# A diagonal LSTM and a small quantum circuit: the resident ring is laid out by runs of eight rows of an image

## The chip, the cores and the metric

The kernel runs on one core of one Trainium2 chip. The metric is the device time in microseconds (us) of one execution; lower is better. Tensors are float32.

## The reference

x has 16 images of 128 channels and 64 x 64 points. Two layers are added to it, each on a group-normalised input (32 groups of four channels):

```
# layer 1: a recurrence along diagonals (rows are skewed: row i is shifted right by i)
xs  = skew(gn(x))                          # 127 columns
i_s = w_is @ xs + b_is                     # 4 gates of 128 channels
for each column t:
    gates = i_s[t] + w_ss[:, :, 0] @ h_of_the_row_above + w_ss[:, :, 1] @ h + b_ss
    o, f, i = sigmoid(...); g = tanh(...)
    c = f * c + i * g;  h = o * tanh(c)
x = x + unskew(h)
# layer 2: at every point, 128 channels -> 4 angles -> circuit of 4 qubits -> 4 values -> 128 channels
x = x + post_w @ simulate(pre_w @ gn(x) + pre_b, q_weights) + post_b
```

## The kernel before

The 128 channels are the partitions. An image has 64 rows of 64 points, 16 KB in a partition, and 16 images are 256 KB, more than fits. So 40 rows of each image stay in an SBUF tile, `ring`, and 24 pass through it in turn. A block is four rows of one image, BLOCK = 256 numbers (1 KB in a partition). `ring` is a tile of [128, 10, 16, 256]: block by block, in each block the 16 images side by side. `block(r)` names the block of row r: rows 32 to 39 lie in blocks 0 and 1, rows 0 to 31 in blocks 2 to 9, and rows 40 to 63 later in blocks 2 to 7. A chunk is 512 numbers, eight rows, in two blocks.

**First stage, loads and statistics (L243 to L430).** For each image, `rows` loads the five chunks of the ring (L246, 80 transfers of 256 KB in all) and `behind` the other three into spare tiles (L259, 48). VectorE takes the statistics of each chunk when it has landed (L283). Beside this, `inv_step` runs 33 serial steps of the recurrence on a state with no input (matmuls L194, activations L197 to L205, products on GpSimd L200 to L202); its results start rows at the border. After the last image come the first products of the gates, three matmuls on loaded rows (`keep`, L177), the group mean (L142) and the inverse root.

**The scan (160 steps, `step`, L743).** All work is ordered by hand. Two bands of 32 rows go along the diagonals, the second 65 steps behind the first. Step t works on one column of each active row: `now`, `new` and the other states have a column per row and image, even rows in one half (q = 0), odd rows in the other, by pairs j. TensorE multiplies by the gates' weights (L583 for the input, L752 for the states); ScalarE and VectorE do the gates. GpSimd, in this order in each step: the differences between neighbouring rows (L605, L608), which TensorE's products need; `residual` (L617), which adds the step before's result to x in the ring; `normalised` (L564, L569, L574), which takes the diagonal of x two steps ahead out of the ring and normalises it. Both walk the ring with `diagonal` (L527): one operation takes a run of row pairs j with all 16 images, and the run is cut where the address pattern demands it. With row blocks of four, a pattern holds an even number of pairs that begins at an even one, and a pair left over at either end is an operation of its own.

When four rows are finished, they are saved to DRAM if the place is needed again (`low`, L629, six times 2 MB), VectorE takes their statistics for the second layer (L705), and then the place is refilled with four further rows of x (L712, six times 2 MB).

**Last stage, the second layer (L956 to the end).** For each image, two halves: angles (L976), sine, the circuit's amplitudes (L1005), squares (L1018), the output product (L1027). `finish` adds the product to the rows on VectorE (L1046) and SyncE sends each chunk to DRAM (L1047). Rows 0 to 23 come back out of `low` into freed places by GpSimd's DMA queue (`load`, L860). Images go in order; the loads run some images ahead.

Of the kernel before, what the change touches and what calls it, by code (L numbers as in the profile page):

```python
# [11 lines left out]
F32 = mybir.dt.float32  # L12
# [4 lines left out]
P = 128  # L17
NB = 16
NH = 64
NW = 64  # L20
# [3 lines left out]
RING = 40  # L24
ROWS = 4
BLOCK = ROWS * NW
CHUNK = 2 * BLOCK
EARLY = 33
FIRST = 8
STRIP = 4  # L30
FEW = 96
LEAST = 128
AHEAD = RING - SLOTS
BAND = NW + 1
# [46 lines left out]
def kernel(  # L81
# [17 lines left out]
    xv = x.rearrange("b c h w -> b c (h w)")  # L99
    ov = out.rearrange("b c h w -> b c (h w)")  # L100

    const = ctx.enter_context(tc.tile_pool(name="const", bufs=1))
# [3 lines left out]

    ring = const.tile([P, RING // ROWS, NB, BLOCK], F32, name="ring")
    NLOW = NH - RING  # L110
    NT = NLOW * NW // CHUNK
    low = dram.tile([NB, P, NLOW * NW], F32, name="low")
# [19 lines left out]
    w_out = const.tile([P, 128], F32, name="w_out")  # L132
    b_out = const.tile([P, 1], F32, name="b_out")

    def block(r):

        return (r + AHEAD if r < SLOTS else r - SLOTS) // ROWS

    def group_mean(psum, v, mean, which, scale):

# [15 lines left out]
    with ExitStack() as scan:  # L156
# [17 lines left out]
        def keep(pool, tag, v):  # L174

            ps = pool.tile([P, v.shape[-1]], F32, name=nc.get_next_instruction_name(), tag=tag)
            nc.tensor.matmul(ps, lhsT=wsT[:, 0:P], rhs=v, start=True, stop=True)  # L177
# [37 lines left out]
        with ExitStack() as prep:  # L215
# [5 lines left out]
            ps_keep = prep_ps.enter_context(tc.tile_pool(name="ps_keep", bufs=1, space=PSUM))  # L221
# [19 lines left out]
            rests = {}  # L241

            def rows(b):  # L243
                for k in ORDERED:
                    at = (2 * k * ROWS - AHEAD) * NW if k else SLOTS * NW
                    nc.sync.dma_start(  # L246
                        out=ring[:, 2 * k : 2 * k + 2, b, :],
                        in_=xv[b, :, at : at + CHUNK].rearrange("c (k n) -> c k n", n=BLOCK),
                    )

            def behind(b):
# [11 lines left out]
            for i in range(2):  # L263
                nc.scalar.dma_start(out=ws_n[i], in_=ws_v[:, 2 * i : 2 * i + 2])
            nc.scalar.dma_start(
                out=qw, in_=q_weights.rearrange("l w a -> (l w a)").partition_broadcast(P)
# [12 lines left out]
            nc.gpsimd.memset(cinv[:, 0:1], 0.0)  # L279

            def statistics(b, k):
                v = ring[:, 2 * k : 2 * k + 2, b, :] if k < 5 else rests[b][k - 5]
                nc.vector.bn_stats(stats[:, b, k, :], v)  # L283

            def aggregated(b):
# [69 lines left out]
            for i in range(2):  # L355
                v = ws_n[i]
# [14 lines left out]
            for b in range(NB):  # L371
                while b < NB - 1 and done * (NB - 1) < EARLY * (b + 1):
                    inv_step(done, ps_inv)
                    keep(ps_keep, "keep", ring[:, 2, b, 0:P])
                    keep(ps_keep, "keep", wsT[:, 0:P])
                    if done == 0:

                        transposed("wxT", wxT, lambda g: wx_n[:, g, :])
                        transposed("w0T", w0T, lambda g: ws_n[g // 2][:, g % 2, 0::2])
                        transposed("w1T", w1T, lambda g: ws_n[g // 2][:, g % 2, 1::2])  # L380
                    elif done > 4 and between:
                        between.pop(0)()
                    done += 1
                if b + 2 < NB:
                    rows(b + 2)
                if b + 1 < NB:
                    behind(b + 1)
                    for k in ORDERED:
                        statistics(b + 1, k)
                for k in (5, 6, 7):  # L390
                    statistics(b, k)
                aggregated(b)
# [134 lines left out]
        def diagonal(t, band, q, j0, j1):  # L527


            j = j0  # L530
            while j < j1:
                odd = (j + AHEAD // 2 * (1 - band)) % 2
                n = 1 if odd or j + 1 == j1 else (j1 - j) // 2 * 2
                r = 2 * j + q + AHEAD * (1 - band)
                at = r // ROWS * NB * BLOCK + r % ROWS * NW + t - BAND * band - 2 * j - q
                dims = [[BLOCK, NB]]
                if n > 1:
                    dims = [[NB * BLOCK - ROWS, n // 2], [2 * NW - 2, 2]] + dims
                yield j, n, bass.AP(origin.tensor, origin.offset + at, [list(origin.ap[0])] + dims)
                j += n  # L540

        def slots(t, band):

            return max(0, t - BAND * band - NW + 1), min(SLOTS, t - BAND * band + 1)

        def over(v, n):
            if n == 1:
                return v
            return v.unsqueeze(1).unsqueeze(1).to_broadcast([P, n // 2, 2, NB])

        def by_pairs(v, q, j, n):
            v = v[:, q, j * NB : (j + n) * NB]
            return v if n == 1 else v.rearrange("p (k h i) -> p k h i", h=2, i=NB)

        def normalised(t):

# [53 lines left out]
        def residual(t, new, engine=nc.gpsimd):  # L610

            for band in range(2):
                s0, s1 = slots(t, band)
                for q in range(2):
                    j0, j1 = (s0 + 1 - q) // 2, (s1 + 1 - q) // 2
                    for j, n, x1 in diagonal(t, band, q, j0, j1):
                        engine.tensor_add(x1, x1, by_pairs(new, q, j, n))  # L617


            for g in range(NG2):  # L620
                done = t - (4 * g + 3 + (-1 if 4 * g < SLOTS else BAND - 1 - SLOTS))
                ends = pieces(g)
                if done in ends:
                    k = ends.index(done)
                    w0 = ends[k - 1] if k else 0
                    waiting.extend((g, k, w0, done, i) for i in range(NB))
                if done == NW:
                    if 4 * g < NLOW:
                        nc.sync.dma_start(  # L629
                            out=low[:, :, 4 * g * NW : (4 * g + 4) * NW].rearrange("b c n -> c b n"),  # L630
                            in_=ring[:, block(4 * g)],
                        )


# [58 lines left out]
        def statistics(us):  # L693

            while waiting:
                g, k, w0, w1, i = waiting[0]
                us -= 0.12 + (w1 - w0) * 0.0035
                if us < 0.0:
                    break
                waiting.pop(0)  # L700
                q = block(4 * g)
                v = ring[:, q, i, :].rearrange("p (r w) -> p r w", w=NW)[:, :, w0:w1]
                if w1 - w0 == NW:
                    v = ring[:, q, i, :]
                nc.vector.bn_stats(stats[:, i, g - FIRST * k, :], v)  # L705
                if i == NB - 1:
                    if g == FIRST - 1:
                        sums.append(early_sums())
                    elif g >= FIRST:
                        sums.append(late_sums(g, k, (w1 - w0) / NW))  # L710
                    if 4 * g < NLOW:
                        nc.sync.dma_start(  # L712
                            out=ring[:, q],
                            in_=xv[:, :, (RING + 4 * g) * NW : (RING + 4 * g + 4) * NW].rearrange(
                                "b c n -> c b n"
                            ),
                        )
# [138 lines left out]

        def low_rows(queue, n, v):
            b, k = n // NT, n % NT
            of = low[b, :, k * CHUNK : (k + 1) * CHUNK]
            queue.dma_start(out=v, in_=of if len(v.shape) == 2 else of.rearrange("p (k n) -> p k n", n=BLOCK))  # L860

        waiting = []
        begin(nc.gpsimd.tensor_copy, cst, 0, cinv, 0)
# [1 line left out]
        with tc.manual_schedule():  # L865
# [23 lines left out]
                add(ps[:, 1], by_one, inner[:, :, h])  # L889
            fill(1)  # L890

            v = ring[:, block(NH - ROWS)].rearrange("p i (r w) -> p i r w", w=NW)[:, :, :, NW - STRIP :]
            d, sq = (work.tile([P, NB, ROWS, STRIP], F32, name=f"strip{i}", tag=f"both{i}") for i in range(2))
            m = mean2.unsqueeze(2).unsqueeze(3).to_broadcast([P, NB, ROWS, STRIP])
            nc.vector.tensor_sub(d, v, m)
# [1 line left out]
            for i, u in enumerate((d, sq)):  # L897
                u = u.rearrange("p i r w -> p i (r w)")
# [57 lines left out]
    def rows_of(b, k):  # L956
        if k < NT:
            return lows[NT * b + k]
        q = block(2 * ROWS * k)
        return ring[:, q : q + 2, b, :]  # L960

    def half(v, c):

        if c is None:
            return v
        return v[:, c] if len(v.shape) == 3 else v[:, c * BLOCK : (c + 1) * BLOCK]

    def bank(pool, name):
        return pool.tile([P, CHUNK], F32, name=name, tag=pool.name)
# [67 lines left out]
    def finish(b, h, po, c=None):  # L1037
        for j in range(4):
            k = 4 * h + j
            v = rows_of(b, k)  # L1040
            x1, y, o = half(v, c), po[j], ov[b, :, k * CHUNK : (k + 1) * CHUNK]
            if c is not None:
                o = o[:, c * BLOCK : (c + 1) * BLOCK]
            elif len(v.shape) == 3:
                y, o = (u.rearrange("p (k n) -> p k n", n=BLOCK) for u in (y, o))
            nc.vector.scalar_tensor_tensor(x1, y, b_out, x1, ALU.add, ALU.add)  # L1046
            nc.sync.dma_start(out=o, in_=x1)  # L1047
            if c != 0:
                places.append(v)
# [97 lines left out]
```

## Time and profile before

| | |
|---|---|
| median of 3 runs | 1421.15 us (1420.26 to 1421.88) |
| the profiled execution | 1419.29 us, its span 1417.5 us, granted TensorE clock 0.994 |
| busy share PE, DVE, ACT, POOL | 95%, 69%, 55%, 65% |
| DMA packets | 91,086; 78,032 of them under 2 KB |
| transfers between ring and DRAM of 256 KB | 80 of x in, 95 of results out, 20 out of `low` |

PE is TensorE's matmul, PEld its weight load, DVE VectorE, ACT ScalarE, POOL GpSimd, SP SyncE, which issues most transfers. The slices of the page divide the span into 40 equal parts of 35.4 us. A digit is a busy share in tenths. A line of the timeline has the start and length in us, the engine, the line of the program and how many instructions are merged; "q" behind an engine is its sequencer, which issues transfers. The DMA view lists packets by size and the time they took as a share of 16 engines. In a view of waits: total in us, times, longest.

### The profile page before, as it was taken

What the parts mean: (1) busy time and instruction counts of PE and PEld (TensorE: products, weight loads), DVE (VectorE), ACT (ScalarE), POOL (GpSimd) and SP (SyncE); (2) the same over time, 40 slices, a digit from 0 to 9 for tenths busy, and PEclk for the clock granted to TensorE, in tenths of its full rate; (3) what the DMA queues carried; (4) which work ended last, traced back from release to release, by engine and by line L of the source; (5) the groups of instructions that cost most, each with busy time, mean ns of one, the idle gap of its engine ahead of it and who ended that gap; (6) DMA issues with size and microseconds to landing.
All of it is one profiled execution on the core that took longest, in us unless ns stands there. A gap on an engine that the chain in (4) does not pass through costs nothing. (4 is left out here: it accounts for less than half of the span.)

```text
span 1417.5 us, 20294 instructions
## 1 busy us (share of the span) xinstructions
PE 1351.7 (95%) x6030; PEld 962.8 (68%) x6030; DVE 980.5 (69%) x2549; ACT 778.3 (55%) x1860; POOL 923.4 (65%) x1823
## 2 busy tenths in 40 slices
PE   6778999999999999999999999999999999989994
PEld 5658887777777677667777667777777788785331
DVE  7993565566665666787777776766665567867994
ACT  4655666555555555555555555555555556644330
POOL 4226787777766667788888766777777677763400
PEclk9999999999999999999999999999999999999997
DMA  9980000000000000133333100000000000005999
GB/s 325 366 284 2 1 2 0 1 1 1 1 0 1 0 1 1 60 119 119 119 119 119 60 1 1 0 1 1 1 1 0 1 1 0 11 22 193 390 371 323
DMA packets 91086, 107.06 MB, mean 76 GB/s; under 512 B 5552, under 2 KB 78032, under 8 KB 90976
## 3 DMA queue, kind: packets, MB, share of 16 engines
q1 hardware_dynamic: 86336, 94.39, 19.7%
q0 software_dynamic: 3408, 10.58, 2.0%
q8 instruction: 48, 0.79, 0.2%
q10 hardware_dynamic: 1232, 0.80, 0.2%
q14 instruction: 62, 0.51, 0.1%
HBM read 59.61 MB, written 46.14 MB: 75 GB/s over the span
## 5 line engine op out<-in xcount | busy, mean ns | idle before, releaser
L583 PE MATMUL ps<-spare,wxT 128*128 128x512 f32 (+18 forms) x1280 | 479.7, 518 | 0.7 <-POOL spare L574 0.7
L767 DVE TENSOR_TENSOR ps<-ps,both 128x256 f32<-128x256 f32 (+9 forms) x544 | 221.5, 408 | 305.2 <-PE ps L752 303.8
L771 ACT ACTIVATE ps<-ps,bias 128x512 f32<-128x512 f32 (+23 forms) x480 | 279.3, 583 | 220.3 <-DVE ps L767 183.7
L752 PE MATMUL ps<-spare,w1T 128*128 128x256 f32 (+16 forms) x1272 | 345.9, 354 | 9.8 <-DVE spare L729 4.9
L583 PEld LDWEIGHTS ps<-spare,wxT 128*128 128x128 f32 x1280 | 231.1, 190 | 173.1 <-issue 155.4
L752 PE MATMUL ps<-spare,w0T 128*128 128x256 f32 (+16 forms) x1272 | 344.0, 352 | 0.8 <-POOL spare L608 0.8
L802 ACT COPY both<-ps 128x256 f32<-128x256 f32 (+9 forms) x544 | 191.4, 354 | 181.1 <-PE ps L752 161.5
L617 POOL TENSOR_TENSOR ring<-ring,spare 128x256 f32<-128x256 f32 (+8 forms) x487 | 247.3, 538 | 31.3 <-DVE stats L705 21.2
L752 PEld LDWEIGHTS ps<-spare,w1T 128*128 128x128 f32 x1272 | 230.0, 190 | 35.5 <-DVE spare L834 7.6
L752 PEld LDWEIGHTS ps<-spare,wsT 128*128 128x128 f32 x1088 | 195.1, 190 | 86.1 <-DVE spare L834 34.6
L752 PE MATMUL ps<-spare,wsT 128*128 128x256 f32 (+14 forms) x1088 | 241.3, 365 | 5.3 <-DVE spare L834 3.6
L752 PEld LDWEIGHTS ps<-spare,w0T 128*128 128x128 f32 x1272 | 230.5, 190 | 22.0 <-POOL spare L608 0.9
L574 POOL TENSOR_TENSOR spare<-spare,rstd 128x512 f32<-128x512 f32 (+10 forms) x160 | 170.8, 1067 | 14.8 <-DVE rstd L153 2.3
L569 POOL TENSOR_TENSOR spare<-ring 128x256 f32<-128x256 f32 (+8 forms) x213 | 146.8, 699 | 0.0
L828 ACT ACTIVATE g<-cst 128x256 f32<-128x256 f32 (+20 forms) x320 | 103.0, 368 | 64.3 <-DVE cst L827 63.7
L834 DVE TENSOR_TENSOR spare<-g,ps 128x256 f32<-128x256 f32 (+17 forms) x319 | 105.4, 368 | 43.8 <-ACT g L828 41.9
L564 POOL TENSOR_TENSOR spare<-ring,mean 128x16 f32<-128x16 f32 (+8 forms) x247 | 130.6, 538 | 6.6 <-DVE mean L143 6.4
L608 POOL TENSOR_TENSOR spare<-spare 128x240 f32<-128x240 f32 (+9 forms) x136 | 102.6, 754 | 29.7 <-DVE spare L834 25.8
L771 ACT ACTIVATE g<-ps,bias 128x512 f32<-128x512 f32 (+20 forms) x160 | 97.3, 608 | 27.1 <-DVE ps L767 21.1
L854 POOL COPY spare<-spare 128x16 f32<-128x16 f32 x64 | 21.0, 329 | 134.6 <-DVE spare L834 134.6
L827 DVE TENSOR_TENSOR cst<-cst,ps 128x256 f32<-128x256 f32 (+20 forms) x320 | 104.5, 368 | 5.5
L824 DVE TENSOR_TENSOR ps<-ps,g 128x512 f32<-128x512 f32 (+20 forms) x160 | 95.0, 594 | 17.0 <-ACT g L771 16.6
(368 smaller groups left out, 1099.7 us busy)
## 6 DMA issues: line engine op xcount, KB each, us to landing
out_dram<-ring SPq DMA_DIRECT2D x95, 256.0 KB, 3.6
ring<-in_x_dram SPq DMA_DIRECT2D x80, 256.0 KB, 5.6
low<-ring SPq DMA_DIRECT2D x6, 2048.0 KB, 7.5
ring<-in_x_dram SPq DMA_DIRECT2D x6, 2048.0 KB, 8.3
spare<-in_x_dram SPq DMA_DIRECT2D x27, 256.0 KB, 5.5
rest<-in_x_dram SPq DMA_DIRECT2D x21, 256.0 KB, 5.6
ring<-low POOLq DMA_DIRECT2D x20, 256.0 KB, 6.6
out_dram<-spare SPq DMA_DIRECT2D x13, 256.0 KB, 4.0
```

The costliest lines, as they stand in the source:

```text
L564: nc.gpsimd.tensor_sub(by_pairs(xn, 0, j, n), x0, over(mean1, n))
L569: nc.gpsimd.tensor_sub(by_pairs(xn, 1, j, n), lower, of)
L574: nc.gpsimd.tensor_mul(v, v, r)
L583: nc.tensor.matmul(ps[g][:, :, a:b], lhsT=wxT[:, g * 128 : (g + 1) * 128], rhs=xns[t % 2][:, :, a:b], start=t > 0, stop=True, skip_group_c ...
L617: engine.tensor_add(x1, x1, by_pairs(new, q, j, n))
L752: nc.tensor.matmul(out, lhsT=w[:, g * 128 : (g + 1) * 128], rhs=rhs, start=False, stop=True, skip_group_check=True,)
L767: nc.vector.tensor_add(v, v, both[g][:, a:b])
L771: nc.scalar.activation(to[:, :, a:w], ps[g][:, :, a:w], FUNC[g], bias=bias[:, g : g + 1])
L802: nc.scalar.copy(both[g][:, a:b], ps[g][:, 0, a:b])
L827: nc.vector.tensor_add(c[:, q], c[:, q], ig[:, q])
L828: nc.scalar.activation(th[:, q, a:w], c[:, q], AF.Tanh)
L834: nc.vector.tensor_mul(new[:, q, a:v], th[:, q, a:v], act[GO][:, q, a:v])
```

## The change

`ring` becomes [128, 5, 16, 512]: the eight rows of two former blocks lie next to each other for each image, 2 KB in a partition. `place(r)` is the former number of the block of four rows; `block(r)` now gives a view, one half of a run of 512. A chunk of an image is one run, so loads of x, results, and chunks coming back out of `low` move 2 KB at a time; saves and refills of four rows still move 1 KB, at a step of 2 KB on the ring's side. `diagonal` cuts its runs at multiples of four pairs: up to three pairs ahead of the first multiple, then a number of whole fours, then up to three pairs. The images of a diagonal lie 2 KB apart, formerly 1 KB.

```diff
-    ring = const.tile([P, RING // ROWS, NB, BLOCK], F32, name="ring")
+    ring = const.tile([P, RING // ROWS // 2, NB, CHUNK], F32, name="ring")
...
+    def place(r):
+        return (r + AHEAD if r < SLOTS else r - SLOTS) // ROWS
+
     def block(r):
-        return (r + AHEAD if r < SLOTS else r - SLOTS) // ROWS
+        q = place(r)
+        return ring[:, q // 2, :, q % 2 * BLOCK : (q % 2 + 1) * BLOCK]
...
                     nc.sync.dma_start(
-                        out=ring[:, 2 * k : 2 * k + 2, b, :],
-                        in_=xv[b, :, at : at + CHUNK].rearrange("c (k n) -> c k n", n=BLOCK),
+                        out=ring[:, k, b, :],
+                        in_=xv[b, :, at : at + CHUNK],
                     )
...
         def diagonal(t, band, q, j0, j1):
+            many = CHUNK // NW // 2
             j = j0
             while j < j1:
-                odd = (j + AHEAD // 2 * (1 - band)) % 2
-                n = 1 if odd or j + 1 == j1 else (j1 - j) // 2 * 2
+                n = min(many - j % many, j1 - j)
+                if n == many:
+                    n = (j1 - j) // many * many
                 r = 2 * j + q + AHEAD * (1 - band)
-                at = r // ROWS * NB * BLOCK + r % ROWS * NW + t - BAND * band - 2 * j - q
-                dims = [[BLOCK, NB]]
-                if n > 1:
-                    dims = [[NB * BLOCK - ROWS, n // 2], [2 * NW - 2, 2]] + dims
+                at = r // (2 * many) * NB * CHUNK + r % (2 * many) * NW + t - BAND * band - 2 * j - q
+                dims = [[2 * NW - 2, min(n, many)], [CHUNK, NB]]
+                if n > many:
+                    dims = [[NB * CHUNK - 2 * many, n // many]] + dims
...
                         nc.sync.dma_start(
                             out=low[:, :, 4 * g * NW : (4 * g + 4) * NW].rearrange("b c n -> c b n"),
-                            in_=ring[:, block(4 * g)],
+                            in_=block(4 * g),
                         )
...
                         nc.sync.dma_start(
-                            out=ring[:, q],
+                            out=block(4 * g),
...
     def rows_of(b, k):
         if k < NT:
             return lows[NT * b + k]
-        q = block(2 * ROWS * k)
-        return ring[:, q : q + 2, b, :]
+        return ring[:, place(2 * ROWS * k) // 2, b, :]
...
-            elif len(v.shape) == 3:
-                y, o = (u.rearrange("p (k n) -> p k n", n=BLOCK) for u in (y, o))
             nc.vector.scalar_tensor_tensor(x1, y, b_out, x1, ALU.add, ALU.add)
             nc.sync.dma_start(out=o, in_=x1)
```

The operands that `normalised` and `residual` pair with a diagonal (`over`, `by_pairs`) are shaped by fours in the same way, and the statistics, the strip at the end and the loads out of `low` take the new views.

## Prediction before the run

> **What bounds the kernel now.** I read the page's slices first, because the change touches three stages that have different limits.
>
> ```profile
> PE   6778999999999999999999999999999999989994
> DVE  7993565566665666787777776766665567867994
> POOL 4226787777766667788888766777777677763400
> DMA  9980000000000000133333100000000000005999
> GB/s 325 366 284 2 1 2 0 1 1 1 1 0 1 0 1 1 60 119 119 119 119 119 60 1 1 0 1 1 1 1 0 1 1 0 11 22 193 390 371 323
> ```
>
> The DMA engines are full in the first three slices (x comes in) and in the last four (results go out). Between them, for over 1,150 us, PE sits at 9 and DMA carries little. So packet size can matter at the two ends only, and the diagonals only in the middle.
>
> The last stage, from the timeline of its end (start, length, engine):
>
> ```profile
> 1396.13 3.38 DVE L1046 SCALAR_TENSOR_TENSOR ring<-po_None,b_out,ring 128x512 f32<-128x512 f32 x5
> ...
> 1409.79 3.67 SPq L1047 DMA_DIRECT2D out_dram<-ring  x5
> ```
>
> VectorE is done at 1399.51, but SyncE issues the last five results only from 1409.79 to 1413.46, and the span ends at 1417.5. The results queue behind the DMA engines; the end is theirs, not an engine's. What a packet costs there is in the DMA view of two stretches: 1382 to 1390, where only results of 1 KB packets go, and 96.9 to 99.3, the drain of the loads into spare tiles, which are 2 KB already.
>
> ```profile
> DMA packets 2844, 2.74 MB, mean 343 GB/s; under 512 B 164, under 2 KB 2844, under 8 KB 2844
> q1 hardware_dynamic: 2844, 2.74, 102.8%
> ```
>
> ```profile
> DMA packets 210, 0.36 MB, mean 152 GB/s; under 512 B 32, under 2 KB 32, under 8 KB 210
> q1 hardware_dynamic: 210, 0.36, 39.7%
> ```
>
> With the tiny semaphore packets taken as free: 1.028 x 16 engines x 8 us / 2680 = 49.1 ns for 1 KB, and 0.397 x 16 x 2.4 us / 178 = 85.6 ns for 2 KB. Two small ones take 98.2.
>
> The first stage, from its timeline, where the loads' end meets another chain:
>
> ```profile
> 94.50 0.29 ACT L205 ACTIVATE hinv<-inv_t,inv_a 128x1 f32<-128x1 f32 x1
> ...
> 98.94 0.91 PE L177 MATMUL I-1407_1408<-spare,wsT 128*128 128x384 f32 x2
> ...
> 100.41 0.37 DVE L286 BATCH_NORM_AGGREGATE mv<-stats 128x2 f32<-128x48 f32 x1
> ...
> 100.88 0.37 PE L142 MATMUL gm<-mv,wide_sb 128*128 128x16 f32 x2 [1.03 <-issue]
> ```
>
> The group mean (L142) waits for the last statistics at 100.78, which follow the loads. But the 33 serial steps of `inv_step` end only at 94.79, and PE then has first gate products and three matmuls on loaded rows until 99.85. The loads lead by 1.03 us, no more.
>
> The scan, by windows (PE, PEld, DVE, ACT, POOL busy), in the two-band part and near its end:
>
> ```profile
> 701.20:709.90 8.70, 8.70 (x35) 6.07 (x34) 6.89 (x20) 4.98 (x11) 7.26 (x17) 1.00 0.01 3
> 1200.00:1240.00 40.00, 36.55 (x239) 31.88 (x237) 33.88 (x130) 24.59 (x74) 29.13 (x70) 1.00 0.03 9
> ```
>
> In the first PE has no gap and POOL 1.44 us of slack in a step; in the second PE is idle 3.45 us of 40, and POOL's lateness can show.
>
> **The change part by part.** *Results.* The page lists 95 transfers out of the ring of 256 KB; each goes from 256 packets to 128. Saved per transfer: 128 x 12.6 ns / 16 engines, divided by an overlap of about 1.05 (shares above 100%), is 0.096 us. The other bound is from the mixed load stretch 20 to 96: its DMA view has 16,679 packets of 1 KB and 5,305 of 2 KB in 107.1% x 16 x 76 us = 1,302 us; with 49.1 for the small, the large cost 91 ns, a pair saves 7.2, a transfer 0.055. Times 95: 9.1 or 5.2 us. I take 8.0, nearer the unmixed row, since the tail is unmixed too. All of it is on the path: the DMA share is 1.02 to 1.07 in every window from 1310 to 1400, and SyncE's last issue, 1412.74, trails VectorE's last result by 13.2 us, more than the saving. VectorE (19.9 of every 20 us busy) and PE keep their pace, so the end cannot come earlier than some 13 us; that floor isn't reached. [...]
>
> [...] The rows above give 13% (85.6 against 98.2), and I go by them.
>
> *Loads of x.* 80 transfers save 0.055 to 0.096 us each, 4.4 to 7.7 us of DMA time. On the path is only the 1.03 us lead; behind it `inv_step` is next (33 steps to 94.79, then PE to 99.85). It could also start later: its weights (512 packets of 1 KB and 128 small ones, 40 on each engine) take turns with x packets that are now 36.5 ns longer, up to 1.5 us. So between 1.0 saved and 0.5 lost; I take 0.3 saved, as some of the x packets are not yet queued in those first microseconds.
>
> *Refills and saves of the ring* (six each, 2 MB, L712 and L629) keep 1 KB packets, since half a block goes at a time: nothing. They land in 8.3 and 7.5 us and are hidden if nothing new waits for them. Statistics, matmuls and additions on whole chunks read one run in place of two: the ring's bn_stats takes 694 ns at most as on spare, and L1046 742 on the ring, 743 on spare: nothing.
>
> *Diagonals.* Walking `diagonal` for all 160 steps, the operations of `normalised` and `residual` go from 979 (the page's L617, L564, L569: 488+247+244) to 1,043. L617 takes 227 ns for 16 columns and 861 for 256, so an operation costs 0.185 us beside its columns. 64 more are 12 us of POOL over the run, unevenly: up to four more in a step (0.74 us) where both bands are ramps. There 7.26 of 8.7 becomes 8.0, still under PE. In steps 138 to 150 it is up to 0.37 us each, 2.9 in all, beside PE's idle time; in 152 to 156 1.7 less; in steps 2 to 7 1.5 less, in 8 to 13 1.4 more. With the cover gone: 4.3 us lost; if only the savings tell: 3.2 gained. I take 0.6 lost, because POOL waits for VectorE more often than the reverse. The larger step along images, 2 KB, isn't in the trace. Nearest rows: contiguous 240 columns (L608) 799 ns, ring 256 columns at 1 KB steps 861, the same per column within 2%; two operands on the ring (L569) 1,074. So 0, and at the outside L569's 25% on one-operand rows, some 0.2 us an operation, which POOL's slack takes.
>
> Sum: -8.0 -0.3 +0.6 = -7.7. The profiled execution took 1419.29 us (span 1417.5 and 1.8 around it) and would take 1411.6; the median of the runs is 1421.15, and becomes **1413.4**.
>
> **The rivals.** *A refill that stalls POOL (slower).* The refill of rows 4g to 4g+3 now shares a block of eight rows with rows still in use by `residual` and `normalised`. If the program's dependencies treat the interleaved halves as overlapping, POOL waits for the landing, 8.3 us, with 4.9 us of its work in that step behind it, and TensorE's next differences (L608) behind that: 8.3 + 4.9 - 7.5 left in the step, about 5.7 us for each of six refills: 34 us, so 1447. It decides from two refills on. For it: a wait that no shared element explains stands in POOL's waits already,
>
> ```profile
> POOL ring L617 <- DVE stats L705: 21.2, 19, 3.5
> ```
>
> a diagonal waiting for statistics of columns already finished. Against: the loads into interleaved images of the ring never wait for the statistics of the image beside them, and a diagonal's pieces now end at block edges, so halves are told apart by a plain step.
>
> *Packets are no cheaper for writes.* The 2 KB results among the small ones (out of `low`) have an issue of 630 ns against 665 and land in 3.4 against 3.5 us: little. If memory sets 347 GB/s, the term is 0 and the time 1421.4, no change. Against: 1320 to 1340, with larger packets mixed in, moved 400.
>
> *POOL's late pieces are on the path* with 4.3 us: 1417.1; it is the upper part of my own case.
>
> **How the numbers follow.** Forecast 0.75, the stall 0.13, no cheaper packets 0.12. Best sum: -9.1 -1.0 -3.2 gives 1407.9, all at once unlikely, so 1409.0; upward the second rival must be inside, 1421.5. That leaves out the stall and a little of the forecast's lower edge. This kernel's runs tell 0.2%, 2.8 us, from no change: faster (under 1418.3) 0.74, within 0.12, slower 0.14.
>
> **What would show it.** Packets of 1 KB fall by 44,800, the count under 2 KB from 78,032 to some 33,200. VectorE's last L1046 still ends about 1399, and SyncE's last issue trails it by 5 us in place of 13; the tail's rate goes from 347 to 385 GB/s or more. The load stage ends near 94, but L142 starts at 99.9 to 101.4. Steps of the two-band part stay at 8.61. Wrong: steps of 12 us or more around 612 to 800 with POOL waiting for a refill; or a tail still at 347 GB/s; or PE idle in 1200 to 1240 over 6 us.

## Result and profile after

| | before | after |
|---|---|---|
| median of 5 runs | 1421.15 us (1420.26 to 1421.95) | 1427.36 us (1425.22 to 1428.36) |
| profiled execution, span, granted clock | 1419.29, 1417.5, 0.994 | 1426.45, 1424.5, 0.991 |

The ratio is 1.0041 (95% interval 1.0027 to 1.0056): 0.41% slower, where 0.5% faster was forecast. The profiled spans differ by 7.0 us. Cut at the first step's product (VectorE's `c * f`, L816 before, L825 after; 105.54 and 103.86 us) and at that of the last step, 159 (1281.77 and 1293.25), they say where:

| stretch | before | after | difference | forecast |
|---|---|---|---|---|
| loads, up to step 0 | 105.54 | 103.86 | -1.7 | -0.3 |
| scan, step 0 to step 159 | 1176.23 | 1189.39 | +13.2 | +0.6 |
| step 159 to the end | 135.73 | 131.25 | -4.5 | -8.0 |

(The lines' numbers move: the refill L712 is now L721, `normalised` L564 and L569 are L574 and L579, `residual` L617 is L627, the differences L605 and L608 are L615 and L618, the statistics L705 are L714, the result's addition L1046 and transfer L1047 are L1051 and L1052.)

The page of the kernel after, DMA's slices and packets:

```profile
DMA  9960000000000000133333100000000000014999
GB/s 339 389 243 1 1 2 0 1 0 1 1 1 1 1 1 1 59 119 119 118 119 119 59 1 1 0 1 1 1 1 1 1 0 1 1 31 146 368 405 352
DMA packets 68686, 107.06 MB, mean 75 GB/s; under 512 B 5552, under 2 KB 33232, under 8 KB 68576
```

The transfers became what the change says: 44,800 packets fewer under 2 KB, higher rates at both ends (the first two slices 339 and 389 GB/s where before had 325 and 366, the last two 405 and 352 where it had 371 and 323). The page's chain of work names the transfer `ring<-in_x_dram` with 2%. GpSimd's waits in the kernel after (total us, times, longest):

```profile
POOL ring L627 <- DVE stats L714: 29.6, 26, 2.3
POOL spare L574 <- DMA ring<-in_x_dram: 16.3, 3, 5.9
```

The second row is new. It is `normalised` waiting for a refill, three times; the first, `residual` waiting for statistics, was 21.2 us before. The timeline around the first refill wait (start, length; in brackets the idle time before and what ended it):

```profile
644.83 0.37 SPq L721 DMA_DIRECT2D ring<-in_x_dram  x1
...
653.16 0.26 POOL L574 TENSOR_TENSOR spare<-ring,mean 128x32 f32<-128x32 f32 x1 [5.07 <-DMA ring<-in_x_dram]
...
655.64 0.69 POOL L618 TENSOR_TENSOR spare<-spare 128x240 f32<-128x240 f32 x1
...
656.38 0.70 PE L761 MATMUL ps<-spare,w0T 128*128 128x256 f32 x2 [2.48 <-POOL spare L618]
```

SyncE issues the refill at 644.83. A piece of 32 columns, two row pairs, waits until it has landed, 8.3 us later. Behind it in GpSimd's order are the rest of `normalised` and the next step's differences (L618), and TensorE stands still for them. Measured from a step's product to the next step's, only three steps grow much: 74 (8.61 to 12.97 us), 82 (to 11.59) and 90 (to 13.12), 11.9 us of the scan's 13.2. All others, but a few next to these or beside statistics, keep their length within 0.1 us. Three refills of the six do it, those of the second half of a block of eight rows, while the lower end of band 1's diagonal still takes a two-pair piece out of the first half. In the kernel before the trace has no such wait.

The stall costs once more. Windows in the kernel after (us, then PE, PEld, DVE, ACT and POOL busy with counts, granted TensorE clock, DMA share, GB/s):

```profile
653.62:657.03 3.41, 0.93 (x5) 0.60 (x4) 0.00 (x0) 0.26 (x1) 3.33 (x9) 1.00 0.00 0
657.03:660.44 3.41, 3.41 (x10) 2.67 (x9) 0.86 (x2) 1.32 (x2) 3.41 (x11) 0.50 0.66 220
```

After 3.41 us in which TensorE was busy for 0.93 us, its granted clock is 0.50 for the next 3.41 us. This happens at 657.03 and 803.80, in two of the three stalls; step 82, which has the same wait and no half clock, is the one that grew least (3.0 us, the others 4.4 and 4.5).

At the end, the timeline and the DMA view of 1392 to 1400, where only results go:

```profile
1410.41 3.38 DVE L1051 SCALAR_TENSOR_TENSOR ring<-po_None,b_out,ring 128x512 f32<-128x512 f32 x5
...
1416.35 3.34 SPq L1052 DMA_DIRECT2D out_dram<-ring  x5
```

```profile
DMA packets 1707, 3.11 MB, mean 389 GB/s; under 512 B 188, under 2 KB 188, under 8 KB 1707
...
q1 hardware_dynamic: 1707, 3.11, 103.1%
```

The last transfer is issued at 1419.09, 5.30 us behind VectorE's last result at 1413.79; it was 13.23. The rate is 389 GB/s, formerly 343. A 2 KB packet takes 1.031 x 16 x 8 us / 1519 = 86.9 ns, near the 85.6 of the forecast.

### The profile page after: what moved, and what is told of

It reads as the page before. It is cut to its first block, busy times and chain, and to the rows that moved or that the text cites. A ratio compares the mean times of both kernels' runs of the same rounds, so it can differ in the third digit from the quotient of the medians.

```text
span 1424.5 us, 20360 instructions
## 1 busy us (share of the span) xinstructions
PE 1357.6 (95%) x6030; PEld 963.3 (68%) x6030; DVE 977.3 (69%) x2549; ACT 778.1 (55%) x1860; POOL 927.5 (65%) x1887
## 4 chain that ended last, share of the span: by engine, by line
PE 77%; DVE 6%; POOL 2%; DMA 2%; ACT 2%; issue 1%; DVEq 0%; ACTq 0%; SPq 0%; POOLq 0%
PE ps L761 44%; PE ps L593 26%; PE po_None L1034 3%; PE theta_None L983 2%; DMA ring<-in_x_dram 2%; PE am_None L1012 1%; DVE spare L843 1%; DVE ps L833 1%; DVE stats L714 1%; DVE ps L776 1%; ACT g L837 1%; DVE cst L836 1%; DVE cst L825 1%; ACT g L780 0%; POOL spare L584 0%
## 5 line engine op out<-in xcount | busy, mean ns | idle before, releaser
L627 POOL TENSOR_TENSOR ring<-ring,spare 128x256 f32<-128x256 f32 (+6 forms) x519 | 251.5, 516 | 42.2 <-DVE stats L714 29.6
L579 POOL TENSOR_TENSOR spare<-ring 128x256 f32<-128x256 f32 (+6 forms) x230 | 149.0, 660 | 0.0
L574 POOL TENSOR_TENSOR spare<-ring,mean 128x256 f32<-128x256 f32 (+6 forms) x263 | 132.8, 515 | 21.9 <-DMA ring<-in_x_dram 16.3
L618 POOL TENSOR_TENSOR spare<-spare 128x240 f32<-128x240 f32 (+9 forms) x136 | 102.4, 753 | 27.6 <-DVE spare L843 23.7
L825 DVE TENSOR_TENSOR cst<-cst,ps 128x512 f32<-128x512 f32 (+20 forms) x160 | 92.8, 580 | 16.4 <-POOL spare L608 10.9
```

What stands on the lines that cost most here:

```text
L574: nc.gpsimd.tensor_sub(by_pairs(xn, 0, j, n), x0, over(mean1, n))
L579: nc.gpsimd.tensor_sub(by_pairs(xn, 1, j, n), lower, of)
```

## The experiments

**Why the refill is waited for.** Theory A: the rows that the piece reads and those that the refill writes are disjoint, but a piece of two pairs (a pattern with a step of 126 elements inside a run of 512) is taken to overlap a refill of the other half of the run. Two kernels test it; the rival B stands in their expectations. In the first, the tails of band 1's diagonal are cut into single pairs:

```diff
                 if n == many:
                     n = (j1 - j) // many * many
+                elif band and n == 2 and j % many == 0:
+                    n = 1
```

> The changed kernel, with one edit in the diagonals: in the second band a run of two pairs at the start of a block of eight rows is cut into two operations of one pair (about 30 more operations on GpSimd). Theory A: the program's dependencies take a pattern of two pairs in one half of a block for overlapping with the refill of the other half, and GpSimd waits 8 us for its landing, three times (refills 1, 3, 5); a single pair is told apart. Then the three waits on the refill (16.3 us in GpSimd's waits) vanish, the steps of 12 to 13 us are 8.61 again, 13.2 us are won: 1414.2 us, between 1411 and 1415. Theory B: the wait is for rows that are really needed, or GpSimd is too long with its further operations: then the waits stay or the steps get longer still, 1427 to 1429 us.

Measured (the kernel before beside it had 1420.49): 1415.97 us (1415.64 to 1417.72), ratio to before 0.9970 (0.9958 to 0.9981), 0.3% faster than before. The scan is 11.4 us shorter than in the kernel after (1189.39 to 1178.00), a little less than A's 13.2, and the time lies 1 us above A's range. No wait for a refill is left; steps 74, 82 and 90 are 8.61 us again, though GpSimd has 32 operations more. Its rows of `residual` and `normalised` in the groups of instructions (count, busy and mean, idle before and what ended it):

```profile
L629 POOL TENSOR_TENSOR ring<-ring,spare 128x256 f32<-128x256 f32 (+6 forms) x535 | 253.9, 506 | 42.3 <-DVE stats L716 29.6 <-DVE spare L845 12.5
...
L576 POOL TENSOR_TENSOR spare<-ring,mean 128x256 f32<-128x256 f32 (+6 forms) x271 | 133.8, 505 | 5.6 <-DVE mean L147 5.4
```

L576 (L574 after) has lost its 16.3 us; L629 still waits 29.6 us for statistics.

In the second, nothing is cut, but the refill is issued behind the step's `normalised`, so that the piece has been read already:

```diff
                     if 4 * g < NLOW:
-                        nc.sync.dma_start(out=block(4 * g), in_=xv[...])
+                        refills.append(g)
...
             if t + 2 < NSTEP:
                 normalised(t + 2)
+            refilled()                    # issues what is in refills
```

> The changed kernel, with the refills issued in program order behind the step's diagonals and not ahead of them; the diagonals as in the change. Theory A (a dependency without a shared element): the diagonals of that step no longer wait for the landing, those of the next step come some 8 us later, when it has landed or nearly so; a wait of at most 1 to 2 us for each refill fits in GpSimd's slack. 1414 us, up to 1417. Theory B (the rows are needed at once): a later refill makes it worse, 1430 us or more.

Measured: 1415.94 us (1415.27 to 1416.73), ratio 0.9970 (0.9959 to 0.9981). GpSimd's waits for refills are small now (the kernel after had 16.3 us):

```profile
POOL spare L574 <- DMA ring<-in_x_dram: 2.6, 3, 1.2
```

Two edits with nothing in common but this wait give the same time, 4.5 us below the kernel before, where the kernel after is 6.2 above it. So the wait is the loss, and it is not one that the data demand, since the piece in single pairs needs no landing. Theory A holds, B falls. That the piece of two pairs is what makes the program's dependencies see an overlap follows from the first edit; how they compare patterns is not shown.

**What a packet is worth in the tail.** Theory P is the forecast's, that packets set the tail's rate; Q its rival. To the split kernel, 60 of the 95 results out of the ring go in 1 KB packets again, with the same bytes and as many transfers (two chunks together, by halves):

```diff
-            nc.sync.dma_start(out=o, in_=x1)
+            if c is None and h:
+                if j % 2:
...
+                    for i in range(2):
+                        s = slice(i * BLOCK, (i + 1) * BLOCK)
+                        nc.sync.dma_start(out=of[:, :, s], in_=ring[:, q : q + 2, b, s])
+            else:
+                nc.sync.dma_start(out=o, in_=x1)
```

> As e1_split, but 60 of the 95 transfers of results out of the ring go by 1 KB packets again: the chunks of the second half of an image are sent two and two, first the first halves of both, then the second halves, the same bytes and the same number of transfers. Theory P (the packets set the tail): each of the 60 costs 0.077 to 0.091 us more, so 4.6 to 5.5 us slower than e1_split, and the tail's rate falls from about 390 to some 360 GB/s. Theory Q (the tail gained by something else, such as fewer descriptors to generate or earlier freed places): within 1 us of e1_split.

Measured: 1419.46 us (1417.91 to 1421.18), 3.5 above the split kernel. The stretch from step 159 to the end, where alone the edit works, goes from 132.06 to 135.49 us, 3.4. That is 0.057 to 0.058 us a transfer. The DMA view of 1392 to 1400, first of the split kernel, then of this one:

```profile
DMA packets 1694, 3.09 MB, mean 387 GB/s; under 512 B 187, under 2 KB 187, under 8 KB 1693
```

```profile
DMA packets 2183, 2.92 MB, mean 366 GB/s; under 512 B 176, under 2 KB 1341, under 8 KB 2182
```

SyncE's last issue trails VectorE by 10.17 us here, by 6.04 in the split kernel. The time is 3.5 us above the split kernel's where Q allows 1, so P holds, at a smaller price than both its own 4.6 to 5.5 and the forecast's: 95 times 0.057 to 0.058 is 5.4 to 5.5 us. The edit also holds the first chunk of each pair back until the second is added; that this costs nothing was not tested, but SyncE is 10.17 us behind VectorE at the end.

**The statistics' waits.** The split kernel still has longer steps: 68 (9.63 us), 76 (9.32), 84 (9.34) and 92 (8.79), each with `residual` waiting for bn_stats. Theory D says that these waits are of the same kind, between the statistics of a finished half and a two-pair piece of the other; E, that they are true.

```diff
-                elif band and n == 2 and j % many == 0:
+                elif n == 2 and j % many == (0 if band else 2):
```

> The split of band 1's two-pair tails, and band 0's two-pair heads (first pair of a run of four is gone, pairs 2 and 3 are left) cut into single pairs too, in the residual and in the normalisation alike. Against the run with the tails alone cut (1415.97 us). Theory D, the waits of the residual for bn_stats in steps 68, 76, 84 and 92 are false ones: the statistics read the first half of a block, the two-pair head adds to the second half, and the two are taken to overlap since its pairs are 126 elements apart. Then these four steps come back to 8.61 us from 9.63, 9.32, 9.34 and 8.79 (step 67 keeps its gain), the residual's time of waiting for DVE stats falls from 29.6 us by about the 4.0 us of those four waits, and the time is 1413.7 to 1414.6. Theory E, the waits are true or those of a statistics queue that is late for another reason: the steps stay, the extra 0.2 us instructions add nothing, 1415.5 to 1416.5.

Measured (before beside it 1420.41): 1413.38 us (1411.04 to 1414.13), ratio 0.9944 (0.9931 to 0.9956), at the lower edge of D's 1413.7 to 1414.6. GpSimd's wait in this kernel:

```profile
POOL ring L629 <- DVE stats L716: 18.7, 18, 1.4
```

The four steps are 8.61 us again, and the scan is 2.5 us shorter than the split kernel's (1175.53 against 1178.00). D holds. The wait fell by 10.9 us, more than the four waits priced: in the split kernel `residual`'s pieces of 32 columns, two pairs, wait eight times in steps 67 to 92, 10.9 us in all, and all eight are gone. The other 18 waits, 18.7 us, lie in steps 100 to 150, at wider pieces (64 to 256 columns). All 19 waits of the kernel before, 21.2 us, lie there too. Whether those are true was not tested. GpSimd has 1,951 operations here, 128 more than before, in a scan 0.7 us shorter than before's.

**The clock at the start of the last stage.** The records show a half clock in every profiled execution of the new layout so far, for 3.41 or 6.83 us, beginning between 1297 and 1301 us (at 1308.98 in the kernel after), and none there in before's. The windows of the last kernel:

```profile
1293.85:1297.26 3.41, 2.37 (x13) 1.51 (x12) 3.12 (x9) 1.76 (x4) 0.00 (x0) 1.00 0.44 154
1297.26:1304.08 6.82, 6.82 (x31) 2.14 (x31) 3.09 (x9) 0.69 (x1) 2.13 (x4) 0.50 0.70 233
```

TensorE's one longer gap there, 1.04 us for a PSUM bank that VectorE frees, is in the kernel before too (first the last kernel, then before):

```profile
1296.61 2.00 PE L1036 MATMUL po<-sq,w_out 32*128 32x256 f32 x6 [1.04 <-DVE ring L1053]
```

```profile
1297.65 1.48 PE L1027 MATMUL po<-sq,w_out 32*128 32x256 f32 x6 [1.04 <-DVE ring L1046]
```

Two idle matmuls fill it, into the bank of an amplitude whose reading is done:

```diff
         for j in range(4):
             k = 32 * j
+            if (b, h, c, j) == (0, 0, 1, 1):
+                am = half(ps_a.tile([P, CHUNK], F32, name="keep_warm", tag="am0"), 0)
+                for _ in range(2):
+                    nc.tensor.matmul(am, lhsT=w_out, rhs=..., start=True, stop=True)
             nc.tensor.matmul(po[j], ...)
```

> As the run with heads and tails split, and two idle matmuls of 256 columns (about 0.44 us each by the fillers in the middle of the program) in TensorE's one gap of 1.04 us in the last stage, between the first and the second output matmul of image 0's second half. Theory F, the half clock that the records show for 3.41 or 6.83 us at the start of the last stage follows a stretch of 3.41 us in which TensorE was busy for 0.69 to 0.81 only: filled, the stretch stands at 0.9 or more, no half clock comes before the end, and the time is 1.5 to 3 us below the run without fillers, at a granted clock of 0.996. Theory G, the clock falls for another reason: the half clock is still there, the time is that of the run without fillers, or up to 0.9 us above it.

Measured: 1411.27 us (1410.81 to 1412.03), ratio to before 0.9931 (0.9918 to 0.9945), 2.1 us below the kernel without fillers. The same stretches of the program:

```profile
1292.70:1296.11 3.41, 3.41 (x17) 2.19 (x16) 3.12 (x9) 1.74 (x4) 0.00 (x0) 1.00 0.44 154
1296.11:1302.93 6.82, 6.82 (x57) 2.07 (x55) 4.71 (x12) 2.79 (x5) 2.13 (x4) 1.00 0.76 240
```

In the same 6.82 us TensorE now starts 57 matmuls instead of 31. Theory F holds here: no half clock is recorded before the program's last matmul has ended (1395.23).

The kernel before with the same fillers and nothing else:

> The kernel before with the same two idle matmuls and nothing else. Theory F: the kernel before loses this clock too in those of its executions whose stretches of 3.41 us fall badly (its runs lie from 1418.39 us at a granted clock of 0.994 to 1421.96 at 0.991; the profiled one had none): filled, its runs draw together at 1417.5 to 1419 us, at a clock of 0.994 or more. Theory G: the median stays at 1420 to 1421 and the spread of 3 us too.

Measured: 1419.19 us (1417.57 to 1421.60), ratio 0.9988 (0.9979 to 0.9996): a gain of 1.2 us, which fits a loss in part of before's executions, but the median lies above F's 1419 and the spread of 4 us stayed. Part of the rest is elsewhere; this kernel's profiled execution has a half clock at the end of the load stage:

```profile
97.45:100.87 3.42, 1.99 (x7) 0.79 (x7) 2.87 (x6) 0.00 (x0) 0.00 (x0) 1.00 0.05 18
100.87:104.29 3.42, 3.42 (x7) 1.67 (x7) 1.93 (x10) 1.50 (x2) 0.58 (x3) 0.50 0.00 0
```

So F is half confirmed for the kernel before; the place with the gap cannot be the only one.

## Why the prediction was wrong

**The step that failed is the refill.** The text gave the refills "nothing" and had them "hidden if nothing new waits for them". Something new did: the pieces of `normalised` that `diagonal` now makes, with three waits of 5.1 to 5.9 us that lengthen the scan by 11.9. The mechanism was named as the first rival, but with 0.13, on the ground that "halves are told apart by a plain step". They are for a single pair; for a piece of two pairs they are not (without this wait alone, 6.2 us above before turn into 4.5 below). The two-pair pieces made a second false wait as well, for statistics, which the sum did not have (steps 68, 76, 84 and 92, 2.5 us of the split kernel's scan). The row that the text showed for the rival, 21.2 us of waits for statistics, is not that wait: it lies in steps 100 to 150, 18.7 us of it are left when the two-pair pieces are gone, and what causes it stays open.

The rival's price was too high. It had six refills at 5.7 us, 34 in all; three stalled, at 4.0 on average. The first half's refills meet only single pairs of the other half at that time (128x16 at 618.08, 692.42 and 764.70 us). And the terms 8.3 + 4.9 - 7.5 took all of GpSimd's work in the step behind the wait, where TensorE only needs it up to the end of L618, 3.2 us after the landing (653.16 to 656.33): 8.3 + 3.2 - 7.5 = 4.0. That this is the measured average is partly luck: the stall without a half clock cost 3.0, and the half clock, which the sum didn't know of, makes up the rest in the other two.

**The results were over-sized.** The mechanism was right, and its marks came: rate, packet time, the trailing issue 5.3 us behind. The term was 8.0, from the unmixed row. Between the two kernels with fillers, neither of which has a half clock there, step 159 to the end goes from 135.8 (before's layout) to 129.9 us: 5.9, that is 0.062 us a transfer, near the 0.057 to 0.058 of the 60 put back to 1 KB and close to the mixed row's 0.055. The trailing issue gains 6.85 of it (13.50 to 6.65 us), but the last transfer takes 1.06 longer from issue to landing (3.17 to 4.23), which the sum left out. In the kernel after only 4.5 was left. There VectorE's last result comes later against step 159 (120.5 us, before 117.7); the half clock at 1308.98 explains it as far as the kernels with and without fillers tell (117.8 and 120.9). The rate in the tail was 343 GB/s with results in 1 KB packets (before, 1382 to 1390) and 387 in 2 KB ones (the split kernel, 1392 to 1400).

**The loads were a little better than forecast,** -1.7 where -1.0 to +0.5 was allowed. The last of x lands at 96.10 us in place of 99.36, 3.3 earlier, but the group mean starts only 1.70 earlier (99.18, marked for 99.9 to 101.4), behind the last matmul on loaded rows:

```profile
98.21 0.91 PE L181 MATMUL I-1407_1408<-spare,wsT 128*128 128x384 f32 x2
99.18 0.30 PEld L146 LDWEIGHTS gm<-mv,wide_sb 128*128 128x128 f32 x2 [0.67 <-PE I-1407_1408 L181]
...
99.18 0.40 PE L146 MATMUL gm<-mv,wide_sb 128*128 128x16 f32 x2
```

The chain behind the loads was named; that `inv_step` would itself end 0.7 earlier was not. Over the six profiles of the new layout the mean starts at 99.1 to 100.5 (average 99.7), over the two of the old one at 100.5 and 100.9, so about 1.0 of it is the layout's, the bound of the range, and the rest is spread.

**GpSimd's operations cost nothing,** not 0.6: with 64 more the steps away from refills and statistics kept their length within 0.1 us, and with 128 more the scan takes 1175.53 us where before's takes 1176.23.

So the sum without the refill is met half way: the split kernel is 4.5 us faster than before where 7.7 was forecast, and with the false statistics' waits gone as well 7.0 (7.9 between the two kernels with fillers, by other terms than the forecast's: 5.9 at the end, 1.0 in the scan, 1.3 in the loads). It needed edits that the change does not have.

## What to carry to other kernels

When two row groups that live at different times are laid into one run, what was told apart by its block must be told apart by its pattern, which the pieces of two pairs here were not (11.9 us of longer steps at three refills): count each transfer into one half, and each statistics operation on it, against each access of several rows to the other half. Price a stall from the landing to the point where the critical engine is served (3.2 us here), not to the end of the waiting engine's step (4.9). Where the end is a queue of transfers, measure a packet's price in the mix that goes there (0.062 us a transfer here, where the forecast's 8.0 for 95 had 0.084), and add what the last one takes to land (1.06 us more here).

## What the runs showed of the hardware

All that follows is read from the records of these runs. The granted clock goes from 1.00 to 0.50 and back, and each half clock that ends again lasts 3.41 or 6.83 us. In the profiled execution of the kernel after, all its changes lie at multiples of 3.413 us from each other (43, 191 and 221 of them from 657.03 to 803.80, 1308.98 and 1411.38). Against the program they fall at other points in other executions: the half clock of the last stage begins 15.5 to 18.0 us behind step 159's product. There it followed a gap of 1.04 us, in a stretch with matmuls of 32 and 64 rows, where TensorE was busy for 0.69 to 0.81 of the 3.41 us ahead of the half clock; that gap is a single wait of TensorE for VectorE. The busy share alone does not decide: at this very gap a stretch at 0.81 (the kernel with 60 results put back) was followed by a half clock and one at 0.79 (before, 1296.9 to 1300.4) by a full one, as was a stretch at 0.49 in the scan of the kernel after (728.7 to 732.1). What is weighed beside it stays open. Two cheap matmuls in the gap were worth 2.1 us in the kernel with heads and tails split, and 1.2 in the kernel before.
